# Query splitting over all partitions and a gather in TensorE's row halves, in a four-layer graph kernel on one core

## The chip, the cores and the metric

The kernel runs on one core of a Trainium2 chip. The metric is the device time of one execution in microseconds. A core has five engines that run side by side, each with its own instruction queue: TensorE (PE, matrix products; its weight loads are listed as PEld), VectorE (DVE), ScalarE (ACT), GpSimd (POOL) and SyncE (SP, which issues most DMAs). They wait for each other by semaphores.

## What is computed

Input `x` is 128 graphs of 64 nodes with 256 features; `adj` is a 64 x 64 matrix. Four graph layers follow one another, each as `x = layernorm(x + layer(x))`. The change touches layer 1 alone:

```python
Xq = (H @ W_lin.T).reshape(bt, n, h, dh)
Xv = (H @ W_val.T).reshape(bt, n, h, dh)
Qs = Xq[:, src]
Kt = Xq[:, dst]
e = jnp.einsum('behd,hd->beh', jax.nn.leaky_relu(Qs + Kt, LRELU_SLOPE), a)
e = e + jnp.log(A0[src, dst] + EPS)[None, :, None]
# softmax of e over the edges of each source node, then
# Y = sum over those edges of attn * Xv[:, dst], and Y @ W_out.T
```

There are 512 edges (`src`, `dst`), 4 heads of 64 features and a slope of 0.2. The leaky Relu is written as a slope times the input plus a rest that a plain Relu gives. For the first part the score of an edge needs only one number per node and head, so four more columns are appended to the query weights (260 columns in all); these are the head columns. For the second part the queries of both ends of each edge must be added for all 256 features, and that sum is a gather: a product with a 0/1 matrix that has a one at the source and at the destination of each edge.

Layer 0 is a dense attention over the 64 nodes, layer 2 two dense products with batch normalisation, layer 3 a graph convolution with four LSTMs.

## The kernel before

Layers 0 and 1, with the first part of layer 2, run in one loop over 16 rounds `q`. A round holds 512 tokens (8 graphs); a chunk `c` of 128 tokens holds two graphs `s`, graph 0 on partitions 0 to 63 and graph 1 on 64 to 127. Each round has eight steps `b`. A step begins with the gather of layer 1 for one graph (`l1_graph(q, b)`, with `c, s = divmod(b, 2)`), and then runs the pieces of other work listed for it in `between`, which belong to other rounds: layer 0 of round q+2, the queries and values of round q+1, the softmax of an earlier pair of rounds, the value products of rounds q-3 and q-4. `step` keeps this order on TensorE, by telling the scheduler to issue each piece after the last TensorE instruction of the piece before. In the first ten steps a setup piece runs as well.

What the eight steps put behind their gather, in TensorE's order (line numbers are those of the profile):

| step | behind the gather |
|---|---|
| 0 | attention times features of layer 0 (L297), 128x128 tiles |
| 1 | head sums (L352), 128x32 tiles; softmax (L371) in even rounds |
| 2 | features of layer 0 (L253), 128x128 |
| 3 | output product of layer 1 (L446), 128x128 |
| 4 | transposes (L227, L395, L264), 128x128 |
| 5 | head sums (L352), 128x32; queries and values of chunks 0 and 1 of round q+1 (L324, L327), 128x128 |
| 6 | aggregation of layer 2 (L467) and values by weights (L432), both 64x64 |
| 7 | transposes of layer 0 (L287); queries and values of chunks 2 and 3 (L324, L327), 128x128 |

`l1_qv` makes the queries `pq` (128 tokens x 260 columns) of a chunk in PSUM. They are taken out in a split form: a rounded part in the type `F32R`, which TensorE multiplies in one pass (a plain `F32` product takes two matmul instructions), and the rest, so that both together keep full precision. `qs` has for graph `s` in `qs[:, s, :]` the rounded part on the graph's own 64 partitions and the rest on the other 64. The matrix `gath_r` holds the 64 x 512 gather matrix twice, one copy on each half of the partitions. One 128-row product then adds rounded part and rest in the array itself (L361). Since the two graphs stand on different halves, ScalarE copies (L334) and VectorE subtracts (L335) once per graph, on 64 partitions each, and ScalarE copies the four head columns of each graph, scaled by the slope, into its place in `spads` (L336). The scheduler lets ScalarE and VectorE read one PSUM bank only one after the other, so these instructions follow each other (L336 stands 17.6 us in all, waiting for L335).

The gather's output `z` takes two PSUM banks and has two buffers; ScalarE evacuates it with a Relu into `u` (L363), 128 x 1024. `reduce_heads` takes four entries `u` off the list `pend`, two steps or more later, and sums over the features of each head into `pes` (L352): four column groups of 32 columns, `n`, are written side by side. `l1_softmax` closes that sum with the product of `spads` (L371). The aggregation of layer 2 uses a buffer of `z` too (L467, evacuated at L471). The other PSUM tiles, `m`, have three buffers, shared by queries, values, transposes and products.

Of the kernel before, what the change touches and what calls it, by code (L numbers as in the profile page):

```python
# [8 lines left out]
F32 = mybir.dt.float32  # L9
F32R = mybir.dt.float32r  # L10
I32 = mybir.dt.int32
AF = mybir.ActivationFunctionType
# [5 lines left out]
P = 128  # L18
NB = 128
N = 64  # L20
D = 256
KD = D // P
HEADS = 4
E = 512
# [6 lines left out]
BPS = 2  # L31
SROWS = BPS * GQ * HEADS
CG = P // PQ
# [4 lines left out]
SLOPE = 0.2  # L38
# [3 lines left out]
def kernel(ctx: ExitStack, tc: tile.TileContext, i, out):  # L42
    nc = tc.nc
# [86 lines left out]
    with ExitStack() as two:  # L130
# [5 lines left out]
        wa = two.enter_context(tc.tile_pool(name="wa", bufs=1))  # L136
# [4 lines left out]
        work = ph.enter_context(tc.tile_pool(name="work", bufs=2))  # L141
        ps = ph.enter_context(tc.tile_pool(name="ps", bufs=1, space=PSUM))

        def bank(shape, name="m", bufs=3):
            return (psm if name == "m" else ps).tile([P] + shape, F32, name=name, bufs=bufs)
# [58 lines left out]
        apad = wa.tile([P, KD, 2 * CG - HEADS], F32, name="apad")  # L204
        gath = wa.tile([P, E], F32, name="gath")
        gath_r = wa.tile([P, E], F32R, name="gath_r")
# [3 lines left out]
        count = wa.tile([P, EC], F32, name="count")  # L210
        place = wa.tile([P, EC], I32, name="place")
        spads = [wa.tile([P, P], F32, name=f"spad{n}") for n in range(2)]


        table = [dram.tile([PAIRS + E, SROWS], F32, name=f"table{n}") for n in range(2)]
# [92 lines left out]
        L1 = {}  # L308
# [5 lines left out]
        def l1_qv(q, c2):  # L314
            xT, v = L1[q]["xT"], L1[q]["v"]

            sp = spads[q // BPS % 2].rearrange("p (s e x b d h) -> p s e x b d h", e=2, s=2, x=2, b=BPS, d=2)
            pv = None
            for c in (2 * c2, 2 * c2 + 1):
                pq = bank([D + HEADS])  # L320
                if pv is None:
                    pv = bank([2, D])
                for k in range(KD):
                    nc.tensor.matmul(pq, xT[:, k, c * P:(c + 1) * P], wq[:, k, :],  # L324
                                     start=k == 0, stop=k == KD - 1)
                for k in range(KD):
                    nc.tensor.matmul(pv[:, c % 2, :], xT[:, k, c * P:(c + 1) * P], wv[:, k, :],  # L327
                                     start=k == 0, stop=k == KD - 1)

                qs = work.tile([P, 2, D], F32R, name="qs", bufs=6)  # L330
                L1[q]["qs"].append(qs)
                for s in range(2):
                    r, ro = slice(s * N, (s + 1) * N), slice((1 - s) * N, (2 - s) * N)
                    nc.scalar.activation(qs[r, s, :], pq[r, :D], AF.Copy)  # L334
                    nc.vector.tensor_sub(qs[ro, s, :], pq[r, :D], qs[r, s, :].bitcast(F32))  # L335
                    nc.scalar.activation(sp[r, s, c % 2, 0, q % BPS, c // 2, :], pq[r, D:], AF.Copy, scale=SLOPE)  # L336
            nc.scalar.activation(v[:, 2 * c2:2 * c2 + 2, :], pv, AF.Copy)

        pes, pend = {}, []
        DEEP = 2  # L340

        def reduce_heads(four):

            q, b, _ = four[0]
            S = q // BPS
            if q % BPS == 0 and b == 0:
                pes[S] = bank([E], name="e", bufs=1)

            for k in range(KD):
                for q, b, u in reversed(four):  # L350
                    n, r0 = b % 2 * 2 + b // 2 % 2, (q % BPS * 2 + b // 4) * HEADS
                    nc.tensor.matmul(pes[S][n * CG:(n + 1) * CG, :],  # L352
                                     apad[:, k, CG - HEADS - r0:2 * CG - HEADS - r0], u[:, k, :],
                                     start=r0 == 0 and k == 0, stop=False)

        def l1_graph(q, b):

            c, s = divmod(b, 2)
            z = bank([KD, E], name="z", bufs=2)
            for k in range(KD):  # L360
                nc.tensor.matmul(z[:, k, :], L1[q]["qs"][c][:, s, k * P:(k + 1) * P], gath_r, start=True, stop=True)  # L361
            u = work.tile([P, KD, E], F32, name="u", bufs=7)
            nc.scalar.activation(u, z, AF.Relu)  # L363
            pend.append((q, b, u))

        ld, sm = {}, {}

# [214 lines left out]
        l0_d(1)  # L582
        l1_t(0)
        l1_qv(0, 0)
        l1_qv(0, 1)


# [91 lines left out]
        def step(do, n, *more):  # L679
            if not 0 <= n < NQ:  # L680
                return
            traced = nc.cur_bb.bb.instructions
            first = len(traced)
            if queue:
                with tc.issue_after(queue[-1]):
                    do(n, *more)
            else:
                do(n, *more)
            mine = [t for t in traced[first:] if t.engine == mybir.EngineType.PE]
            queue.extend(mine[-1:])  # L690

        def behind(do, q):
            if q < NQ:
                with tc.issue_after([t for t in nc.cur_bb.bb.instructions
                                     if t.engine == mybir.EngineType.Activation][-1]):
                    do(q)

        def sums(q):
            reduce_heads([pend.pop(0) for _ in range(min(4, len(pend)))])

        for q in range(NQ):
            S = q // BPS - 1 if q % BPS == 0 else -1
            between = [
                [(l0_e, q + 1), (l0_a, q + 2)],
                [(sums, q if q else -1), (l1_softmax, S)],
                [(l1_sums, S), (l0_b, q + 2)],
                [(v_b, q - LAG - 1)],
                [(l1_t, q + 1), (l1_weights, S), (l0_c, q + 2)] + [(l0_x, q + 2)] * (S < 0),
                [(sums, q), (l1_qv, q + 1, 0)] + [(lambda n: behind(l0_x, n), q + 2)] * (S >= 0),
                [(v_c, q - LAG - 1), (v_a, q - LAG)],  # L710
                [(l0_d, q + 2), (l1_qv, q + 1, 1)],
            ]
            for b in range(GQ):
                step(l1_graph, q, b)
                for do, n, *more in between[b]:
                    step(do, n, *more)
                if setup:
                    setup.pop(0)()
        sums(q)
        S = NQ // BPS - 1  # L720
# [256 lines left out]
        q = NQ - LAST - 1  # L977
# [199 lines left out]
    work = ctx.enter_context(tc.tile_pool(name="work3", bufs=2, reuse_waits="tile"))  # L1177
# [752 lines left out]
    for k in range(NP):  # L1930
# [5 lines left out]
        for n in range(2):  # L1936
            g = k * 2 + n
            for s in range(SKIP - 1):
                u = 34 + 4 * s + 2 * n
# [65 lines left out]
```

## Time and profile before

| | us |
|---|---|
| median of 3 runs | 2036.22 |
| lowest, highest | 2034.6, 2041.47 |
| the profiled execution | 2039.12 |
| its span, from first to last instruction | 2037.3 |
| first gather starts (L361) | 52.9 |
| last gather starts | 518.0 |

| in the changed code | count | mean or median ns |
|---|---|---|
| gather, L361, 128x512 | 256 | 480 |
| Relu, L363, 128x1024 | 128 | 1026 |
| query copy, L334, 64x256 | 128 | 379 |
| subtraction, L335, 64x256 | 128 | 422 |
| head copy, L336, 64x4 | 128 | 168 |
| head sums, L352, 128x32 tiles | 512 | 607 |

The duration of a matmul in such a profile is modelled, from the issue to the end of its pass through the array, and neighbours overlap; how fast a stream runs is read from the starts of neighbours. PEld is the loading of a matmul's weights into the array, which can run beside the matmul before. A form such as `64*128` is the tile of the array that an instruction uses: rows times columns. An idle stretch stands in brackets with what ended it.

### The profile page before, as it was taken

How to read it: one execution, taken by the hardware profiler on the slowest of the kernel's cores; microseconds unless marked ns; L12 is line 12 of the kernel's file. 1: busy time of each engine (PE TensorE's matmuls, PEld its weight loads, DVE VectorE, ACT ScalarE, POOL GpSimd, SP SyncE). 2: the span in 40 equal slices, each digit the busy share in tenths (PEclk: the TensorE clock that was granted, in tenths of full speed). 3: DMA queues.
4: the chain of work that ended last, by engine and by line, in shares of the span. 5: the costliest groups of instructions: out<-in, count | busy, mean ns of one | idle time of the engine just before them, and what ended most of it. 6: DMA issues, size and time to landing. Idle time of an engine off the chain costs nothing.

```text
span 2037.3 us, 31496 instructions
## 1 busy us (share of the span) xinstructions
PE 1940.1 (95%) x11447; PEld 1337.8 (66%) x11447; DVE 1248.0 (61%) x2763; ACT 988.0 (48%) x1892; POOL 880.0 (43%) x1017
## 2 busy tenths in 40 slices
PE   5999999999999999899999999999999999999996
PEld 4667777766554445477678577667577668578685
DVE  7456565565456555765557865557775557664566
ACT  2766666666345633644343644333544333543333
POOL 1123333333445544564645543435543445444264
PEclk8999999999999998999999999999999999999999
DMA  5344443332302025433243243133143032132022
GB/s 129 85 67 65 83 68 55 66 45 39 51 22 60 38 93 185 148 139 107 86 162 92 66 155 136 39 132 88 58 152 121 24 111 66 47 119 78 0 62 73
DMA packets 236539, 173.84 MB, mean 85 GB/s; under 512 B 150624, under 2 KB 213600, under 8 KB 233056
## 3 DMA queue, kind: packets, MB, share of 16 engines
q1 hardware_dynamic: 234528, 169.86, 29.5%
q8 instruction: 90, 1.47, 0.3%
q0 software_dynamic: 1024, 1.05, 0.2%
q10 hardware_dynamic: 832, 0.92, 0.1%
q14 instruction: 65, 0.53, 0.1%
HBM read 110.18 MB, written 61.60 MB: 84 GB/s over the span
## 4 chain that ended last, share of the span: by engine, by line
PE 73%; DVE 14%; ACT 5%; DMA 3%; issue 3%; POOL 2%; SPq 1%; DVEq 0%; POOLq 0%; ACTq 0%
PE l L1728 27%; PE l L1684 8%; PE pz L845 4%; PE l L1463 4%; PE m L253 3%; PE pz L774 3%; PE m L324 3%; PE e L352 2%; PE m L446 2%; PE g L1362 2%; PE m L327 2%; PE z L361 2%; PE g L1350 2%; PE pz L1043 2%; DVE cell L1642 1%
## 5 line engine op out<-in xcount | busy, mean ns | idle before, releaser
L1728 PE MATMUL l<-hs,wh 128*128 128x256 f32 (+1 forms) x896 | 276.0, 399 | 3.7 <-DVE hs L1592 3.1
L1728 PE MATMUL l<-xs,wx 128*128 128x256 f32 (+1 forms) x896 | 276.2, 399 | 2.9 <-DVE gate L1747 2.7
L1743 ACT ACTIVATE kept<-l 128x256 f32<-128x256 f32 (+1 forms) x224 | 88.8, 403 | 333.2 <-PE l L1728 331.8
L86 POOL TENSOR_TENSOR ln_rs<-ln_rs,mhalf 128x2 f32<-128x2 f32 (+2 forms) x98 | 85.5, 873 | 367.4 <-DVE ln_rs L98 366.9
L1728 PE MATMUL l<-H,wx 128*128 128x256 f32 (+1 forms) x672 | 210.5, 402 | 4.3 <-DVE gate L1756 3.4
L1728 PE MATMUL l<-hid,wh 128*128 128x256 f32 (+1 forms) x672 | 208.7, 399 | 0.0
L1728 PEld LDWEIGHTS l<-hs,wh 128*128 128x128 f32 x896 | 169.1, 190 | 47.1 <-DVE hs L1592 5.7
L1728 PEld LDWEIGHTS l<-xs,wx 128*128 128x128 f32 x896 | 168.9, 190 | 46.1 <-issue 2.8
L1761 ACT ACTIVATE gate<-gate,bias 128x512 f32<-128x512 f32 (+1 forms) x280 | 170.6, 657 | 40.7 <-DVE gate L1752 34.8
L1684 PE MATMUL l<-H,wx 128*128 128x256 f32 (+5 forms) x672 | 185.2, 431 | 4.9 <-DVE H L116 2.7
L363 ACT ACTIVATE u<-z 128x1024 f32<-128x1024 f32 x128 | 130.3, 1026 | 68.8 <-PE z L361 67.7
L1684 PEld LDWEIGHTS l<-H,wx 128*128 128x128 f32 x672 | 118.8, 190 | 65.5 <-issue 34.2
L1728 PEld LDWEIGHTS l<-H,wx 128*128 128x128 f32 x672 | 125.7, 190 | 42.6 <-DVE gate L1756 7.4
L1728 PEld LDWEIGHTS l<-hid,wh 128*128 128x128 f32 x672 | 127.2, 190 | 32.0 <-issue 2.9
L1751 POOL TENSOR_TENSOR gate<-gate,kept 128x256 f32<-128x256 f32 (+1 forms) x84 | 65.1, 775 | 144.9 <-DVE kept L1749 136.2
L335 DVE TENSOR_TENSOR qs<-m,qs 64x256 fp32r<-64x256 f32 x128 | 54.0, 422 | 106.3 <-ACT qs L334 104.4
L361 PE MATMUL z<-gath_r,qs 128*128 128x512 f32 x256 | 100.4, 480 | 9.3 <-ACT u L363 8.9
L1756 DVE TENSOR_TENSOR gate<-l,gate 128x256 f32<-128x256 f32 (+1 forms) x112 | 50.0, 446 | 88.4 <-POOL gate L1751 64.3
L1596 POOL TENSOR_TENSOR hs<-hid 128x256 f32<-128x256 f32 (+1 forms) x28 | 26.0, 929 | 170.1 <-DVE hid L1628 87.0
L1650 ACT ACTIVATE gate<-cell 128x512 f32<-128x512 f32 (+1 forms) x88 | 58.6, 666 | 83.6 <-DVE cell L1642 61.5
L1638 POOL TENSOR_TENSOR cell<-gate,cell 128x512 f32<-128x512 f32 (+1 forms) x56 | 75.4, 1367 | 28.4 <-ACT gate L1761 28.4
L1745 DVE TENSOR_TENSOR gate<-l,kept 128x256 f32<-128x256 f32 (+1 forms) x112 | 49.1, 438 | 59.7 <-ACT gate L1761 32.6
(380 smaller groups left out, 4097.6 us busy)
## 6 DMA issues: line engine op xcount, KB each, us to landing
wx<-sums SPq DMA_DIRECT2D x9, 2048.0 KB
wh<-sums SPq DMA_DIRECT2D x9, 1792.0 KB
way<-st SPq DMA_DIRECT2D x54, 256.0 KB
st<-way SPq DMA_DIRECT2D x216, 64.0 KB
xin<-in_x SPq DMA_DIRECT2D x16, 512.0 KB
ld<-table SPq DMA_DIRECT2D x16, 512.0 KB
x_dram<-y SPq DMA_DIRECT2D x16, 512.0 KB
x2r<-x_dram SPq DMA_DIRECT2D x32, 256.0 KB
```

Of the source, the lines that this page charges most:

```text
L86: nc.gpsimd.tensor_tensor(dst, dst, mhalf[:, :n], OP.pow)
L253: nc.tensor.matmul(p_, xT[:, k, c * P:(c + 1) * P], w0[:, k, :], start=k == 0, stop=k == KD - 1)
L361: nc.tensor.matmul(z[:, k, :], L1[q]["qs"][c][:, s, k * P:(k + 1) * P], gath_r, start=True, stop=True)
L363: nc.scalar.activation(u, z, AF.Relu)
L845: nc.tensor.matmul(self.bank[at], lhs, rhs, start=first and n == 0, stop=n == len(self.terms) - 1, skip_group_check=True)
L1463: nc.tensor.matmul(self.bank[at], lhs, rhs, start=new, stop=True, skip_group_check=True)
L1638: nc.gpsimd.tensor_tensor(c, t, c, OP.mult)
L1684: nc.tensor.matmul(b, w.raw[0][:, k, at, m, :], x, start=k == 0, stop=k == KD - 1)
L1728: nc.tensor.matmul(self.banks[j], lhs, rhs, start=src == 0, stop=src == 1)
L1743: nc.scalar.activation(self.keep(j), b, AF.Copy)
L1751: e.tensor_tensor(t[0][:, 1], t[0][:, 1], k[5], OP.add)
L1761: given(lambda: nc.scalar.activation(dst, dst, f, bias=b))
```

## The change

The queries of a chunk are split for all 128 partitions at once: `qs[:, 0, :]` is the rounded part of both graphs, `qs[:, 1, :]` the rest. A rounded part and its rest are now on the same partitions, in two places of the free dimension. So the gather takes 64 rows at a time: graph `s` uses the rows `s * 64` to `s * 64 + 63` of `qs` and of `gath_r`, and the two parts are two products that accumulate in PSUM. A step no longer makes one graph with two blocks of 128 features, but one block `k` of both graphs: four products of 64 rows and 512 columns, two for each row half. `z` and `u` now have the graph where the feature block was. `reduce_heads` takes its four entries in the new order and writes the same column groups. The head columns go into `spads` by one VectorE product per chunk, of the four columns with a mask `slopes`, which holds the slope where partition and graph belong together and zero elsewhere; GpSimd writes the mask once.

```diff
--- before.py
+++ after.py
@@ -210,6 +210,10 @@
         count = wa.tile([P, EC], F32, name="count")
         place = wa.tile([P, EC], I32, name="place")
         spads = [wa.tile([P, P], F32, name=f"spad{n}") for n in range(2)]
+        slopes = wa.tile([P, 2, HEADS], F32, name="slopes")
+        nc.gpsimd.memset(slopes, 0.0)
+        for s in range(2):
+            nc.gpsimd.memset(slopes[s * N:(s + 1) * N, s, :], SLOPE)
 
 
         table = [dram.tile([PAIRS + E, SROWS], F32, name=f"table{n}") for n in range(2)]
@@ -329,11 +333,10 @@
 
                 qs = work.tile([P, 2, D], F32R, name="qs", bufs=6)
                 L1[q]["qs"].append(qs)
-                for s in range(2):
-                    r, ro = slice(s * N, (s + 1) * N), slice((1 - s) * N, (2 - s) * N)
-                    nc.scalar.activation(qs[r, s, :], pq[r, :D], AF.Copy)
-                    nc.vector.tensor_sub(qs[ro, s, :], pq[r, :D], qs[r, s, :].bitcast(F32))
-                    nc.scalar.activation(sp[r, s, c % 2, 0, q % BPS, c // 2, :], pq[r, D:], AF.Copy, scale=SLOPE)
+                nc.scalar.activation(qs[:, 0, :], pq[:, :D], AF.Copy)
+                nc.vector.tensor_sub(qs[:, 1, :], pq[:, :D], qs[:, 0, :].bitcast(F32))
+                nc.vector.tensor_mul(sp[:, :, c % 2, 0, q % BPS, c // 2, :],
+                                     pq[:, None, D:].to_broadcast([P, 2, HEADS]), slopes)
             nc.scalar.activation(v[:, 2 * c2:2 * c2 + 2, :], pv, AF.Copy)
 
         pes, pend = {}, []
@@ -341,27 +344,31 @@
 
         def reduce_heads(four):
 
-            q, b, _ = four[0]
+            q, c, _, _ = four[0]
             S = q // BPS
-            if q % BPS == 0 and b == 0:
+            if q % BPS == 0 and c == 0:
                 pes[S] = bank([E], name="e", bufs=1)
-
+            r0 = (q % BPS * 2 + c // 2) * HEADS
             for k in range(KD):
-                for q, b, u in reversed(four):
-                    n, r0 = b % 2 * 2 + b // 2 % 2, (q % BPS * 2 + b // 4) * HEADS
-                    nc.tensor.matmul(pes[S][n * CG:(n + 1) * CG, :],
-                                     apad[:, k, CG - HEADS - r0:2 * CG - HEADS - r0], u[:, k, :],
-                                     start=r0 == 0 and k == 0, stop=False)
-
-        def l1_graph(q, b):
-
-            c, s = divmod(b, 2)
-            z = bank([KD, E], name="z", bufs=2)
-            for k in range(KD):
-                nc.tensor.matmul(z[:, k, :], L1[q]["qs"][c][:, s, k * P:(k + 1) * P], gath_r, start=True, stop=True)
-            u = work.tile([P, KD, E], F32, name="u", bufs=7)
+                for _, c, _, u in [part for part in reversed(four) if part[2] == k]:
+                    for s in range(2):
+                        n = s * 2 + c % 2
+                        nc.tensor.matmul(pes[S][n * CG:(n + 1) * CG, :],
+                                         apad[:, k, CG - HEADS - r0:2 * CG - HEADS - r0], u[:, s, :],
+                                         start=r0 == 0 and k == 0, stop=False)
+
+        def l1_edges(q, ck):
+
+            c, k = divmod(ck, KD)
+            z = bank([2, E], name="z", bufs=2)
+            for part in range(2):
+                for s in range(2):
+                    r = slice(s * N, (s + 1) * N)
+                    nc.tensor.matmul(z[:, s, :], L1[q]["qs"][c][r, part, k * P:(k + 1) * P],
+                                     gath_r[r, :], start=part == 0, stop=part == 1)
+            u = work.tile([P, 2, E], F32, name="u", bufs=7)
             nc.scalar.activation(u, z, AF.Relu)
-            pend.append((q, b, u))
+            pend.append((q, c, k, u))
 
         ld, sm = {}, {}
 
@@ -711,7 +718,7 @@
                 [(l0_d, q + 2), (l1_qv, q + 1, 1)],
             ]
             for b in range(GQ):
-                step(l1_graph, q, b)
+                step(l1_edges, q, b)
                 for do, n, *more in between[b]:
                     step(do, n, *more)
                 if setup:
```

## The prediction

> **What bounds the kernel now.** First the page's totals, then the totals of the stretch that runs the changed code (52 to 520 us), then who waits for whom in its steady part, then single instructions in order of time.
>
> ```profile
> span 2037.3 us, 31496 instructions
> PE 1940.1 (95%) x11447; PEld 1337.8 (66%) x11447; DVE 1248.0 (61%) x2763; ACT 988.0 (48%) x1892; POOL 880.0 (43%) x1017
> ```
> ```profile
> 52.00:520.00 468.00, 438.35 (x3699) 316.58 (x3703) 263.45 (x678) 313.38 (x686) 155.16 (x177) 0.98 0.36 63
> ```
> The second line's columns: stretch, length, then busy time of PE, PEld, DVE, ACT and POOL. PE is busy 94% of it, ACT 67%, DVE 56%. So TensorE is the bound, and time saved elsewhere counts only where PE waits. The waits of PE from 160 to 470 us, ten of the sixteen rounds:
>
> ```profile
> PE z L361 <- ACT u L363: 8.6, 5, 1.8
> PE m L324 <- ACT yT L436: 4.0, 10, 0.6
> PE m L395 <- ACT tT L228: 1.5, 5, 0.3
> ```
> All three end on ScalarE: 14.1 us that a lighter ScalarE could give back at best. The longest, in one round:
>
> ```profile
> 306.36 0.38 ACT L334 ACTIVATE qs<-m 64x256 fp32r<-64x256 f32 x1 [1.90 <-PE m L324]
> 307.22 0.17 ACT L336 ACTIVATE spad<-m 64x4 f32<-64x4 f32 x1 [0.49 <-DVE qs L335]
> ...
> 312.12 1.02 ACT L363 ACTIVATE u<-z 128x1024 f32<-128x1024 f32 x1
> ```
> ```profile
> 313.20 0.73 PE L361 MATMUL z<-gath_r,qs 128*128 128x512 f32 x2 [1.76 <-ACT u L363]
> ```
> The Relu of step 6 starts only at 312.12 behind four query copies, four head copies and four exponentials; step 7's gather needs its bank and PE stands for 1.76 us.
>
> Next, what a change of TensorE's tile shape costs, since the change adds many. Into another shape:
>
> ```profile
> 320.78 0.40 PE L361 MATMUL z<-gath_r,qs 128*128 128x512 f32 x1
> 321.10 0.62 PE L352 MATMUL e<-u,apad 128*32 128x512 f32 x1
> ```
> Into the whole array after an idle stretch, then on in the same shape:
>
> ```profile
> 322.96 0.30 PEld L361 LDWEIGHTS z<-gath_r,qs 128*128 128x128 f32 x2 [0.84 <-ACT u L363]
> 323.30 0.42 PEld L253 LDWEIGHTS m<-w,tT 128*128 128x128 f32 x2
> ```
> ```profile
> 322.96 0.73 PE L361 MATMUL z<-gath_r,qs 128*128 128x512 f32 x2
> 323.53 0.38 PE L253 MATMUL m<-w,tT 128*128 128x258 f32 x1
> ```
> Out of row halves (64*128), which stand once in the trace, in the setup at L644:
>
> ```profile
> 67.72 0.59 PE L644 MATMUL m<-A 64*128 64x512 f32 x1
> 68.23 0.33 PE L227 MATMUL m<-ident,A 128*128 128x128 f32 x1
> ```
> L253's load starts as the second gather does, so the first gather took 323.30 - 322.96 = 0.34 and the second 323.53 - 323.30 = 0.23 us. The 0.11 between them is a weight load that nothing hides. In the first fence the successor comes 0.32 us after the gather instead of 0.23: 0.09 of emptying. In the last, a pass of 512 columns of plain f32 streams 0.43 us (groups at L352 follow each other by that), the successor's load starts 68.23 - 67.72 = 0.51 after it: 0.08 of emptying, and then that load is in the open. The data it waits for by semaphore, POOL's L100, had ended at 67.17.
>
> **What the Trainium skill says.** "TensorEngine Tiling (Array Packing)", Tiling Modes, Key Properties: changing the tiling mode, not merely the tile, drains TensorE. It lists 64x128 as a mode of its own; the 0.08 to 0.09 us above agree. "TensorE: Matmul & The Clock Gate", LDWEIGHTS: a load costs its columns over 1.2, whatever the rows, so 128 columns take 107 ns; the trace's 0.11 agrees. Same page, Part 3 (Packing small matmuls): tiles in different row groups start some 4 ns apart and run together. The 64*64 groups at L467 agree: 64 matmuls start within 1.0 us, 15 ns each, in fours.
>
> **The change part by part.**
> *Query copies.* Per 128 tokens before: two ACT copies (379 ns each, L334), two DVE subtractions (422, L335), two ACT head copies (168, L336). After: one ACT copy, one subtraction, one DVE product of 128x8. Partitions don't lengthen an instruction: ACT copies 128x258 in 382 ns at L255. So I keep 0.38 and 0.42. The product is not in the trace; the smallest DVE rows take 164 (L96) to 178 ns (L281), a PSUM source of 128x128 329 (L267). I take 0.18, with 0.16 and 0.33 as ends. Over 64 chunks ACT loses 64 x (379 + 2 x 168) = 46 us of work; DVE 64 x 422 - 64 x 180 = 15 us. Behind the product on DVE stand layer norms and the next transpose; DVE has 44% free, so nobody waits. ACT stops waiting for DVE between its own copies. None of this is PE's time; it pays in PE's waits alone.
>
> *What PE gets back.* In even rounds, ACT's queue between 306.36 and 312.12 after the change holds a copy, a copy at 308.1, the copy of v (ready 308.96) to 309.6, and 1.8 us of exponentials: the Relu starts near 311.35, 0.8 earlier. Six such waits: 4.8. In odd rounds (1.43 us of copies fewer ahead of the same Relu) L324's wait for yT, 0.56, shrinks by some 0.45: seven, 3.2. The wait at L395 for tT shrinks by 0.2 behind a later L227: seven, 1.4. At the start (52.08) L324 waits 2.39 us for the last head copy to free a bank; with copy, subtraction and product the bank is free some 1.4 sooner. Sum: 10.8 us.
>
> *The gathers.* 256 of 128x512 become 512 of 64x512, in pairs on the two row halves, each half with its own bank of z. If the halves run together, a step streams 2 x 0.23 us as before: zero. The second part's loads go beside the first part's stream, as L467's do.
>
> *The switches.* Each step now goes into 64*128 and out. Counted along the timeline, shapes change 94 times in layers 0 and 1 before, 260 after: per round two more at steps 0, 3 and 4 (neighbours 128*128), one or two at step 2, one each at 1, 5 (column tiles follow), 6 (64*64 follow) and 7 (64*64 before); fewer in the first four and last two rounds. So 166 more. Each costs 0.09 + 0.11, for gathers up to 0.02 more: 0.21 us, together 34.9. Cover: at step 7, fourteen exits fall into L324's wait for yT, 2.9; before 160 us PE waits for other chains, where I put 2.0. Without either cover the loss is the whole 34.9. Ends for a switch: 0.16 (row loads partly beside the old stream) and 0.24.
>
> *The rest.* reduce_heads issues the same 512 matmuls over four distinct column groups, in another order, on data a step and more old (it takes the first four of six entries): zero. No DMA is added, removed or moved; SP's queue is as before. POOL gets three memsets at its start, 0.1 us each by its row for 128x1, ahead of work that next runs at 9.76: zero.
>
> *Sum.* +34.9 - 4.9 - 10.8 = +19 us. Span 2037.3 to 2056; the profiled execution, 2039.1, to 2058; it stands 2.9 above the median of the runs, 2036.2, so there 2055.
>
> **The rivals.**
> *A, switches into row halves are free.* Then only the gain stays: 2036.2 - 10.8 = 2025. For it: full columns stay in use, entry at L644 (67.18, 0.32 after the last gather) also had semaphores to pass. Against it: the clean exit above, and the skill's rule. This is the faster side; it decides from a switch under 0.065 us (10.8 / 166), three tenths of what I take.
> *B, the halves don't run together.* 256 more streams of 0.23, 59 us, on top: 2036 + 19 + 59 = 2114. Against it: L467, though in plain f32 and 64 columns wide; a 512-wide one-pass gather writes PSUM at twice that pace per tile.
> *C, the relief of ACT reaches all of PE's waits* (14.1 us in ten rounds, some 20 in all) and switches cost 0.16: 26.6 - 20 = +6, 2042. With drains, no gain in the profile can cross zero.
>
> **How the numbers follow.** Forecast with its own range 2042 to 2068 (switch 0.16 with 16 us back; 0.24 with 6 back): 0.74, C being its lower end. A: 0.17. B: 0.05. Undetermined, near no change: 0.04. Ends: 2024 to 2072 leave out B and tails. A measurement here tells 0.3%, 6 us, from no change. Faster 0.19, same 0.06, slower 0.75.
>
> **What would show it.** In the new profile: gathers of 64*128 in pairs a few ns apart (else B); 0.3 us or more from a step's last gather to a following 128*128 load (else A); step 7's 1.76 near 0.8; ACT's busy time down by some 46 us; stage end near 540 instead of 520 us. If ACT falls by 46 and the end of the stage comes earlier, my switch price is wrong.

## The result, and the profile after

The changed kernel takes 2043.37 us in the median of 13 runs, the kernel before 2040.28 on the same chips. The ratio is 1.0022, with a 95% interval of 1.0012 to 1.0032: some 4 us slower, clear of no change in these runs, though less than the 0.3% that the prediction took for the least that can be told from it. The forecast was 19 us slower. The execution profiled took 2043.14 us.

The page's totals, and the totals of the same stretch as before (stretch, length, busy time of PE, PEld, DVE, ACT and POOL, granted share of TensorE's clock, busy share of the DMA engines, GB/s):

```profile
span 2041.4 us, 31869 instructions
PE 1957.4 (96%) x11703; PEld 1323.3 (65%) x11703; DVE 1225.7 (60%) x2763; ACT 945.9 (46%) x1700; POOL 880.8 (43%) x1020
```
```profile
52.00:520.00 468.00, 451.97 (x3811) 298.26 (x3809) 241.04 (x671) 267.68 (x490) 154.80 (x173) 0.99 0.36 61
```
ScalarE lost 988.0 - 945.9 = 42 us of work and VectorE 1248.0 - 1225.7 = 22, where 46 and 15 were forecast. PE's busy share of the stretch rose from 94% to 97%: it waits less, and needs more time for the same products. The last gather starts at 525.4 us, 7 us later than before; the prediction put the end of this stage 20 us later. The instructions that take out the queries, from the groups by line and form (count, then busy time and mean ns):

```profile
L337 DVE TENSOR_TENSOR qs<-m,qs 128x256 fp32r<-128x256 f32 x64 | 27.2, 424 | 96.8 <-ACT qs L336 96.0
L336 ACT ACTIVATE qs<-m 128x256 fp32r<-128x256 f32 x64 | 24.9, 389 | 50.1 <-PE m L328 50.0
L338 DVE TENSOR_TENSOR spad<-m,slopes 128x8 f32<-128x8 f32 x64 | 9.9, 155 | 0.0
```
The copy and the subtraction on 128 partitions take what they took on 64 (379 and 422 ns), and the product 155 ns, just below the lower end set for it.

The whole list of PE's waits from 160 to 470 us (in all, times, longest), where there were three kinds and 14.1 us. The wait of step 7, for which the prediction gave 0.8 us, is down to 0.4:

```profile
PE z L367 <- ACT u L370: 2.0, 5, 0.4
```

Now one visit to the row halves, in order of time, matmuls first and then weight loads:

```profile
285.31 0.38 PE L331 MATMUL m<-wv,tT 128*128 128x256 f32 x1
285.62 0.50 PE L367 MATMUL z<-gath_r,qs 64*128 64x512 f32 x2
...
285.96 0.40 PE L367 MATMUL z<-gath_r,qs 64*128 64x512 f32 x2
286.29 0.48 PE L301 MATMUL m<-wh,eT 128*128 128x256 f32 x1
```
```profile
285.62 0.30 PEld L367 LDWEIGHTS z<-gath_r,qs 64*128 64x128 f32 x4 [0.33 <-issue]
286.29 0.73 PEld L301 LDWEIGHTS m<-wh,eT 128*128 128x128 f32 x4 [0.37 <-issue]
```
The gathers come in pairs: two of 64 rows begin at 285.62 and last together 0.50 us, as one of them does, and the next pair begins at 285.96. So the halves run together. On both sides the drain stands open: the first row load comes 0.31 us after the last 128x128 matmul, which streams for 0.22 (L327 and L446 follow each other by that), and L301's load 0.33 us after the second pair, which streams for some 0.23 (the 0.34 from pair to pair, less the 0.11 of a load that nothing hides). Each time the load itself, 0.11 us, follows before the array works again. From start to start along these two shape changes the way became 0.40 us longer than before, 0.20 for one; the prediction took 0.21.

### The profile page after: what moved, and what is told of

Its sections match the earlier page's. It is cut to its first block, busy times and chain, and to the rows that moved or that the text cites. A ratio compares the mean times of both kernels' runs of the same rounds, so it can differ in the third digit from the quotient of the medians.

```text
span 2041.4 us, 31869 instructions
## 1 busy us (share of the span) xinstructions
PE 1957.4 (96%) x11703; PEld 1323.3 (65%) x11703; DVE 1225.7 (60%) x2763; ACT 945.9 (46%) x1700; POOL 880.8 (43%) x1020
## 4 chain that ended last, share of the span: by engine, by line
PE 76%; DVE 14%; ACT 3%; DMA 3%; issue 2%; POOL 2%; SPq 0%; DVEq 0%; POOLq 0%; ACTq 0%
PE l L1735 27%; PE l L1691 7%; PE pz L852 4%; PE l L1470 4%; PE z L367 3%; PE pz L781 3%; PE m L257 3%; PE m L328 3%; PE e L356 3%; PE m L331 2%; PE m L453 2%; PE g L1369 2%; PE pz L1050 2%; PE g L1357 2%; PE m L301 1%
## 5 line engine op out<-in xcount | busy, mean ns | idle before, releaser
L367 PE MATMUL z<-gath_r,qs 64*128 64x512 f32 x512 | 92.4, 443 | 2.0 <-ACT u L370 2.0
L337 DVE TENSOR_TENSOR qs<-m,qs 128x256 fp32r<-128x256 f32 x64 | 27.2, 424 | 96.8 <-ACT qs L336 96.0
```

Of the source, the lines that this page charges most:

```text
L367: nc.tensor.matmul(z[:, s, :], L1[q]["qs"][c][r, part, k * P:(k + 1) * P], gath_r[r, :], start=part == 0, stop=part == 1)
```

## Where the time went: a ledger of eight rounds

The span falls into three parts: up to the first value product (L432 before, L439 after), which stands near the end of the fourth round, from there eight full rounds, and the rest. All numbers are differences of starts in the traces, in us:

| profiled execution | before the eight rounds | eight rounds | rest of the span |
|---|---|---|---|
| before | 157.4 | 245.05 | 1634.9 |
| changed | 155.1 | 249.56 | 1636.7 |
| relief alone | 147.6 | 234.22 | 1631.8 |
| rows alone | 162.4 | 257.92 | 1639.1 |
| mask alone | 150.8 | 238.81 | 1633.4 |
| four pairs | 153.2 | 242.14 | 1635.5 |
| three pairs | 153.9 | 240.86 | 1631.2 |
| wide copy | 150.8 | 234.22 | 1632.2 |
| one copy, VectorE's second | 151.3 | 234.21 | 1631.7 |

Within the eight rounds TensorE's time from start to start can be split. A group of matmuls between the same neighbours takes the same time in every round when it doesn't wait; the least value of each, summed, is the work, and what is over is called waiting here. Before: 226.7 of work and 18.3 of waiting, with 48 changes of tile shape. Changed: 244.3 and 5.3, with 140 changes. So 92 more changes added 17.6 us, 0.191 each, and the waits gave 13.1 back. This split is an estimate: it depends on which groups are taken as alike, and other choices give 0.17 to 0.24 for a change. The 0.40 us of the visit above, read from single starts, lies between. Some 3 us of the 18.3 are no wait but a slower clock, as the first experiment shows.

## The experiments

Each is compared with the kernel before on the same chip. Two theories stood. W: the price of a switch was right, and PE's waits on ScalarE were about twice what the prediction counted. S: the waits were as counted, and most switches cost nothing. They differ in what the relief of ScalarE is worth by itself. The cuts of code below leave out the lines that make the mask `slopes`, which are those of the changed kernel.

### The relief alone

The kernel before with the new copies, and the gather left at 128 rows. This kernel leaves the layer's sum out: its gather adds parts of two graphs, where it should add the rounded part and the rest of one. TensorE has the same instructions as before, so it serves to measure the time:

```diff
-                for s in range(2):
-                    r, ro = slice(s * N, (s + 1) * N), slice((1 - s) * N, (2 - s) * N)
-                    nc.scalar.activation(qs[r, s, :], pq[r, :D], AF.Copy)
-                    nc.vector.tensor_sub(qs[ro, s, :], pq[r, :D], qs[r, s, :].bitcast(F32))
-                    nc.scalar.activation(sp[r, s, c % 2, 0, q % BPS, c // 2, :], pq[r, D:], AF.Copy, scale=SLOPE)
+                nc.scalar.activation(qs[:, 0, :], pq[:, :D], AF.Copy)
+                nc.vector.tensor_sub(qs[:, 1, :], pq[:, :D], qs[:, 0, :].bitcast(F32))
+                nc.vector.tensor_mul(sp[:, :, c % 2, 0, q % BPS, c // 2, :],
+                                     pq[:, None, D:].to_broadcast([P, 2, HEADS]), slopes)
```

> The kernel before with the new query split and mask (one ACT copy, one subtraction, one product per chunk) but the old gather over 128 rows, so no tile switch is added. The gather then adds up parts of both graphs; its instructions, shapes and waits are those of before. Theory W (TensorE's waits on ScalarE were twice what I counted, with stretches at half clock that they set off): 22 to 30 us faster than before, ratio 0.985 to 0.989, no half-clock stretch between 100 and 450 us. Theory S (the waits were as counted, and most switches cost nothing): 11 us faster, ratio 0.9945.

Ratio 0.9900 (0.9886 to 0.9914): 20.4 us faster. That is just short of W's 22 and far from S's 11, which lies outside the interval. PE's busy time from 160 to 470 us, the kernel before first and then this one:

```profile
160.00:470.00 310.00, 295.63 (x2706) 219.79 (x2705) 185.15 (x478) 207.29 (x462) 114.69 (x131) 0.99 0.35 63
```
```profile
160.00:470.00 310.00, 303.41 (x2808) 225.48 (x2810) 182.00 (x500) 181.50 (x346) 124.30 (x141) 0.99 0.38 65
```
With the same matmuls, PE does 2808 of them in the time of 2706. By tile, the 10.8 us of the eight rounds went from these starts: the value products and the wait behind them for the Relu, 5.8; the transposes of L287 behind which L324 waits for yT, 3.3; queries and values, 3.5; and the aggregation took 1.9 more, waiting now for its own input. The 3.5 is mostly not a wait. The granted clock, the last but two of the columns, in the kernel before and then in the changed kernel, in the same four microseconds:

```profile
252.00:256.00 4.00, 3.78 (x11) 2.95 (x10) 0.46 (x2) 3.13 (x7) 1.21 (x2) 0.57 0.03 8
```
```profile
252.00:256.00 4.00, 3.92 (x18) 2.87 (x16) 0.73 (x3) 2.77 (x6) 0.96 (x1) 1.00 0.05 12
```
In the kernel before TensorE ran at half clock for 3.4 us from 252.3 and again from 375.1, each time just after a wait of 1.8 us at step 7 (250.96 and 373.99); each time eight matmuls took some 1.6 us longer than elsewhere. With the relief alone and in the changed kernel there is no such stretch in these rounds. W expected none between 100 and 450 us with the relief alone; there was one, at 116.7, outside the eight rounds.

Nearly as much lies ahead of them: 157.4 - 147.6 = 9.8 us. Before (ScalarE's timeline, VectorE's, then PE's):

```profile
50.42 0.17 ACT L336 ACTIVATE spad<-m 64x4 f32<-64x4 f32 x1 [3.33 <-DVE qs L335]
```
```profile
49.18 0.75 DVE L623 TENSOR_SCALAR_CACHE_REDUCE A<-A 128x512 f32<-128x512 f32 x1
...
49.97 0.42 DVE L335 TENSOR_TENSOR qs<-m,qs 64x256 fp32r<-64x256 f32 x1
```
```profile
52.08 1.14 PE L324 MATMUL m<-wq,tT 128*128 128x260 f32 x4 [2.39 <-ACT spad L336]
...
71.87 1.92 PE L352 MATMUL e<-u,apad 128*32 128x512 f32 x16
```
With the relief alone:

```profile
48.81 1.11 PE L328 MATMUL m<-wq,tT 128*128 128x260 f32 x4 [1.16 <-DVE spad L338]
...
66.73 1.93 PE L355 MATMUL e<-u,apad 128*32 128x512 f32 x16
```
From 44 to 51 us VectorE is full of setup work (L623), and a subtraction waits for its place in VectorE's queue, and ScalarE for the subtraction. A chunk is handed from ScalarE to VectorE or back four times before and once with the relief, and the first head sums start 5.1 us sooner. Some 1.7 us of that is clock again: before, the clock granted from 54 to 58 us is 0.57, with the relief 1.00. How the other 4.7 of the 9.8 us came about is not shown.

### The row halves alone

The changed kernel with the copies of before, each on 64 partitions:

```diff
-                nc.scalar.activation(qs[:, 0, :], pq[:, :D], AF.Copy)
-                nc.vector.tensor_sub(qs[:, 1, :], pq[:, :D], qs[:, 0, :].bitcast(F32))
-                nc.vector.tensor_mul(sp[:, :, c % 2, 0, q % BPS, c // 2, :],
-                                     pq[:, None, D:].to_broadcast([P, 2, HEADS]), slopes)
+                for s in range(2):
+                    r = slice(s * N, (s + 1) * N)
+                    nc.scalar.activation(qs[r, 0, :], pq[r, :D], AF.Copy)
+                    nc.vector.tensor_sub(qs[r, 1, :], pq[r, :D], qs[r, 0, :].bitcast(F32))
+                    nc.scalar.activation(sp[r, s, c % 2, 0, q % BPS, c // 2, :], pq[r, D:], AF.Copy, scale=SLOPE)
```

> The changed kernel with the copies of before (per graph: an ACT copy, a subtraction and an ACT head copy, on 64 partitions), so the row-half gather with all its switches but no relief of ScalarE. Theory W: the switches add 33 us of TensorE's own time, and a later TensorE waits less for an unchanged ScalarE, by 10 to 20 us: 13 to 23 us slower than before, ratio 1.006 to 1.011. Theory S: what the change lost, 3 + 11 = 14 us or less: ratio 1.007 or less, with switches that cost under 0.1 us each in the trace's starts.

Ratio 1.0106 (1.0092 to 1.0119): 21.6 us slower, as W had it at its upper end. PE's waits on ScalarE from 160 to 470 us:

```profile
PE z L364 <- ACT u L367: 5.5, 5, 1.4
PE m L324 <- ACT yT L440: 1.1, 4, 0.3
```
The waits on ScalarE fell from 14.1 to 6.6 us though ScalarE does all it did before: a PE that comes later finds it done sooner. In the eight rounds 12.9 of the 17.6 us of switches came through; 1.6 of the difference is the clock, with one stretch at half clock there (0.57 granted from 391 to 395 us) in place of two. Over the kernel, 163 more switches (94 before, 257 after, in the trace) at 0.191 are 31 us, and 21.6 came through, so some 10 were covered, mostly by old waits.

Relief and rows together would be 21.6 - 20.4 = +1.2; the change gave +4.5, a difference that the intervals of the three ratios allow. In the eight rounds of the traces it is 12.87 - 10.83 = +2.0 against +4.5. So the two don't quite add, as one would expect: a wait that one of them takes away isn't there for the other.

### The mask alone

The kernel before, with the two head copies of a chunk replaced by the product:

```diff
-                    nc.scalar.activation(sp[r, s, c % 2, 0, q % BPS, c // 2, :], pq[r, D:], AF.Copy, scale=SLOPE)
+                nc.vector.tensor_mul(sp[:, :, c % 2, 0, q % BPS, c // 2, :],
+                                     pq[:, None, D:].to_broadcast([P, 2, HEADS]), slopes)
```

> The kernel before with the head columns alone changed: one VectorE product through the mask per chunk, in place of two ACT head copies. No switch is added. ScalarE loses 128 x 0.168 = 21.5 us of its 46, and half its waits for VectorE. Theory W: about half of the relief, 8 to 15 us faster, ratio 0.993 to 0.996. Theory S: 5 us faster, ratio 0.9975.

Ratio 0.9954 (0.9941 to 0.9967): 9.4 us faster, inside W's range and past S's 5. The head columns, 4 of 260, carry nearly half of the gain of all the relief, and their copies were nearly half of the work taken off ScalarE (21.5 of 46 us). Each small copy also makes ScalarE wait for VectorE; what that is worth by itself is not shown. Of the 6.2 us that the eight rounds gained, 2.9 stand at queries and values, where the two stretches at half clock are gone here too.

### Fewer visits to the row halves

The changed kernel with the gathers of two steps together:

```diff
-                step(l1_edges, q, b)
+                if b % 2:
+                    step(l1_edges, q, b - 1)
+                    step(l1_edges, q, b)
```

> The changed kernel with the gathers of two steps run one behind the other at every odd step, none at even steps: four visits to the row halves a round in place of eight, 6.5 switches fewer a round, some 95 in all. Theory W: 95 x 0.19 = 18 us faster than the changed kernel, less what the second gather of a pair waits for a free z buffer (0 to 0.5 us in 64 pairs): ratio to before 0.991 to 1.000. Theory S: switches are nearly free, so no gain, and the buffer waits make it slower: ratio 1.002 to 1.015.

Ratio 0.9987 (0.9981 to 0.9994), so 0.9987 / 1.0022 = 0.9965 of the changed kernel: 7 us, where 18 were expected less what is lost at z. In the eight rounds 52 switches fewer took some 9 us of work away, 0.175 each. The waits from 160 to 470 us:

```profile
PE z L367 <- ACT A L478: 2.1, 5, 0.4
PE m L328 <- ACT eT L293: 1.1, 5, 0.2
```
Step 7 now needs both z buffers just behind the aggregation, which uses one, and two Relus in a row put off eT. So a variant keeps steps 6 and 7 single:

```diff
-                step(l1_edges, q, b)
+                if b in (1, 3, 5):
+                    step(l1_edges, q, b - 1)
+                if b not in (0, 2, 4):
+                    step(l1_edges, q, b)
```

> The changed kernel with gathers paired at steps 1, 3 and 5, and single at steps 6 and 7: five visits to the row halves a round. Compared with four pairs there is one switch more a round (3 us), but step 7 no longer needs the z buffer of the aggregation at once, so its waits there (0.34 us a round) and behind it for eT (0.4 us a round) go: 12 us. Theory W: 5 to 9 us faster than four pairs, ratio to before 0.994 to 0.997. If the waits at step 7 do not go, ratio 0.999 to 1.001.

Ratio 0.9974 (0.9964 to 0.9983): some 3 us faster than four pairs (1.3 in the eight rounds), hardly more than the two intervals allow, and not the 5 to 9 of the expectation. The waits for eT and for A are gone; one for the Relu is there:

```profile
PE z L367 <- ACT u L370: 2.1, 5, 0.4
```
Both runs show that switches cost time and that their number can be halved. Neither reaches what the relief gives without any.

### The relief without the row halves

Two ways to relieve ScalarE and keep the 128-row gather, with each graph's rounded part and rest on opposite halves. One writes the rounded part of all 128 partitions to both places at once and lays the rests over it:

```diff
+                nc.scalar.activation(qs, pq[:, None, :D].to_broadcast([P, 2, D]), AF.Copy)
                 for s in range(2):
                     r, ro = slice(s * N, (s + 1) * N), slice((1 - s) * N, (2 - s) * N)
-                    nc.scalar.activation(qs[r, s, :], pq[r, :D], AF.Copy)
                     nc.vector.tensor_sub(qs[ro, s, :], pq[r, :D], qs[r, s, :].bitcast(F32))
-                    nc.scalar.activation(sp[r, s, c % 2, 0, q % BPS, c // 2, :], pq[r, D:], AF.Copy, scale=SLOPE)
+                nc.vector.tensor_mul(sp[:, :, c % 2, 0, q % BPS, c // 2, :],
+                                     pq[:, None, D:].to_broadcast([P, 2, HEADS]), slopes)
```

> The kernel before with the mask, and with both ACT query copies of a chunk made one: a copy of 128 partitions written to both places of qs (128x512), over which the two subtractions lay their rests. The gather stays at 128 rows, no switch is added. ScalarE loses 64 x (2 x 0.379 + 2 x 0.168 - 0.60) = 32 us in place of 46. Theory W (relief pays about 0.45 us for each us that ScalarE loses, as in the runs with relief and with the mask alone): 13 to 18 us faster than before, ratio 0.991 to 0.9935. Theory S: 7 us, ratio 0.9965.

Ratio 0.9917 (0.9903 to 0.9930): 16.9 us faster than before. The copy of 128x512 takes 0.60 us, as expected.

The other has ScalarE copy once and VectorE place the second graph's part:

```diff
+                nc.scalar.activation(qs[:, 0, :], pq[:, :D], AF.Copy)
+                nc.vector.tensor_copy(qs[N:, 1, :], qs[N:, 0, :])
+                for s in (1, 0):
+                    r, ro = slice(s * N, (s + 1) * N), slice((1 - s) * N, (2 - s) * N)
+                    nc.vector.tensor_sub(qs[ro, s, :], pq[r, :D], qs[r, s, :].bitcast(F32))
...
```

> The kernel before with the mask and one ACT copy of 128x256 per chunk; VectorE copies the second graph's rounded half to its other place and makes both rests. The gather stays at 128 rows. ScalarE is relieved as in the changed kernel (46 us), VectorE gets a copy of 64x256 and the product more. Theory W: as relief alone, 17 to 21 us faster, ratio 0.9895 to 0.9915, unless VectorE's longer chain delays a bank: then up to 5 us less. Theory S: 11 us, ratio 0.9945.

Ratio 0.9922 (0.9908 to 0.9936), a little less than expected, and no different from the wide copy. The table shows where the rest stays: both need 234.2 us for the eight rounds, exactly what the relief alone needs, and lose 3 to 4 us to it ahead of them. VectorE is full of setup work there and has one or two instructions more a chunk than with the relief alone, which is the likely cause but was not tested. Once ScalarE is rid of 32 us, ridding it of more gives nothing in full rounds. These two are the fastest versions that compute the whole layer, 17 and 16 us under the kernel before and some 20 under the changed one.

## Why the prediction missed

The direction was right: the halves run together, each visit drains the array twice, and the drains cost a little more than the relief returns. The sum was wrong, +19 against +3 (medians) to +4.5 (ratio), through these terms:

- **What PE gets back, 10.8 us: the step that failed.** The relief alone measured 20.4 (23.7 between the two profiled executions; that of the kernel before took 2039.1 us, 3 more than the median that the ratio rests on). The prediction took the waits listed for ten full rounds, extended them to thirteen or fourteen, and allowed 1.4 for the start. By the traces the relief took 9.8 ahead of the eight rounds, some 8 more than allowed; 10.8 in them, where the forecast comes to 3.2 + 1.8 + 0.8 = 5.8; and 3.1 behind them, about what was left for it. In the eight rounds step 7 and the aggregation gave 3.9 net (forecast 3.2), the wait for yT behind L287 3.3 (forecast 1.8), and the wait at L395 for tT nothing (forecast 0.8; 1.2 us in the list both before and with the relief alone). Another 3.5 came from queries and values, most of it from two stretches at half clock that I didn't look for. The page's row of granted clock doesn't show them: it has a 9 in each of these slices.
- **The switches, 34.9 us.** 163 at 0.191 are 31. The price of 0.21 was some 10% high by this measure; the count was three too high.
- **Their cover, 4.9 us.** Some 10 with ScalarE as before: a second step that was sized too small. I counted as cover only waits that stood next to a switch. The waits for yT, which I did count, fell by 2.9 in the ten rounds; but those for the Relu at step 7 fell by 3.1 as well, and those for tT, 1.5, went altogether, with no switch beside the transposes that wait. A wait on another engine can shrink by the switches that stand anywhere ahead of it.
- **The rows at nothing held**: pairs of gathers, head sums, mask product and memsets cost what was said, or less.

Rival A (switches free) is refuted by the run with rows alone; B (halves one after the other) by the starts of the pairs. C had named the cause in part, that all of PE's waits are reached, some 20 us; with the measured price of a switch in place of its 0.16 it still sums to +11, because the cover was missing. That its +6 came close to the measured change is luck: a price too low stood in for the cover.

Not shown is what sets off the half clock. In the nine traces, from 50 to 430 us, it was granted 16 times, and each time the stretch began during a wait of TensorE of 1.3 us or more, or within 2.3 us behind it. But 15 other waits as long had none: at step 7 of the eight rounds before, two of four (1.5 to 1.8 us) were followed by one; with the rows alone one of two (1.34 and 1.36), and with the mask alone, which keeps one of 1.5, none. No run puts such a wait in or out by itself.

## What to carry to other kernels

When one engine is relieved and another pays, measure the two halves of the change apart: here -20 and +22 us stood behind a change of +4, and most of the cheap half, -17 us, could be had alone. Before a matmul is cut into a tile shape of its own, count the changes of shape in TensorE's order; here 163 of them, at 0.19 us each, made 31 us of TensorE's time, of which 21.6 came through. And read the waits of a bound engine by the starts of its instructions and over the start of the kernel as well: in the eight rounds the list of waits, which goes by modelled ends, held 11.5 us before the change, where the starts show 18.3 (some 3 of it from the slower clock), and 9.8 more could be had ahead of them.

## What the runs showed of the hardware

- A row-half tile of all columns drains TensorE as a change of columns does: some 0.1 us of emptying and 0.11 us of an open load at each of its two ends in the visit shown, some 0.19 us a change on average. The Trainium skill's rule in "TensorEngine Tiling (Array Packing)", Tiling Modes, Key Properties, that a change of mode drains and a change of tile doesn't, holds for these shapes: the two matmuls of one pair, in different tiles, start within 0.01 us of each other.
- Waits of TensorE of 1.8 us were followed by 3.4 us at half clock twice in the eight rounds before (0.57 granted over 252 to 256 us), and one of 1.3 us once with the rows alone (0.57 over 391 to 395 us); as many waits of that length were not. No list of waits shows it.
- A product of 128x8 on VectorE with PSUM as a source took 155 ns, less than the small SBUF rows by which the prediction priced it (164 to 178).
